# A decoder layer with a selective scan: decays in two SBUF tiles, one scan per step, C's rows in PSUM, normalisation on ScalarE

## The chip, the core and the metric

The kernel runs on one core of a Trainium2 chip. A core has five engines with an instruction queue each: TensorE (PE in the profile; its weight loads are PEld), VectorE (DVE), ScalarE (ACT), GpSimd (POOL) and SyncE (SP), which here only issues DMA transfers. Each engine works through its queue in order; semaphores make one engine wait for another. SBUF is the memory that all engines and the DMA reach, PSUM the small one that TensorE writes its results to. The metric is the time of one execution on the device, in microseconds (us), as the median of several runs.

## What is computed

x is 64 sequences of 128 tokens with 512 channels. Three blocks follow each other, each on a normalised x and added to it: a state-space block (1024 inner channels, 16 states each), an attention block in a band of 64 tokens either way, with a second input that multiplies its result, and a mixture of eight small experts of which two are taken. The part that the change touches most is the first:

```python
def ssm_block(x):                       # x normalised
    h_in, gate = split(x @ in_proj_w.T)
    u   = silu(causal_conv(h_in, 4 taps))
    ts, B, C = split(u @ x_proj_w.T)    # 128, 16, 16 wide
    dt  = softplus(ts @ dt_proj_w.T + dt_proj_b)
    dA  = exp(dt[..., None] * -exp(A_log))
    h_t = dA_t * h_(t-1) + (dt * u)[..., None] * B     # along the tokens
    y   = sum over the 16 states of h * C, plus D * u
    return (y * silu(gate)) @ out_proj_w.T
```

## The kernel before

Two sequences form a group (`GB` = 2, so 256 columns, `TG`); there are 32 groups. The 1024 channels times 16 states of a group are worked off in 32 steps, so 1024 steps in all. Step k belongs to group g, to a block ib of 128 channels and to a quarter j of the states (`where`, line 258). In a step, 128 partitions carry 32 channels times 4 states, and the free dimension 4 quarters of the block times 256 columns, 1024 elements.

A step has these parts, each a function with a line that shows in the profile:

- `loads` (262): once per block, two DMA transfers from scratch in DRAM spread dt (tile dtr) and dt times u (dur) over the partitions. Each has two tiles.
- `by_b` (line 279): GpSimd multiplies dur by B's rows (brep) into h, which has two tiles.
- `decays` (292): ScalarE writes exp(dt A) into da. da lies in PSUM: two halves of 512 elements, one tile each, used by every step again. The first column of each sequence stays zero, which starts the recurrence anew.
- `scan` (300): VectorE runs the recurrence over one half, in place in h. There are two scans per step.
- `by_c` (309): VectorE multiplies h by C's rows (crep, SBUF) into hc; right behind it stand the matmuls that sum over the states into yp (314, 319).
- `gated` (328): once per block VectorE multiplies yp by the gate into y.

All other work is written as four generators, "strands": strand_b makes the next group's inputs (`front`: normalisation, in-projection pin, convolution u, silu th on ScalarE and GpSimd, projections, brep and crep, softplus e, lo, ln, dt), strand_c the gates (pg, gt), strand_a the out-projection po and the attention, strand_t the attention's end (`tail`: o, pw, y2, pc) and the experts. They yield after each piece with a number of ticks to pass and sometimes a condition. The main loop puts eight ticks into every step, and what is due is issued there. So the order on each engine is fixed when the program is built: for step k it is by_b of k+1, first scan, first half of the decays of k+1, two ticks, second scan, second half, gated of k-1, two ticks, by_c with its matmuls, four ticks. One PSUM tile, ps_b, serves one after another most products of the strands; a strand waits with its next product until it is given back (`take_b`, `give_b`).

Normalisation, three times per group: `moments` on VectorE (359, 360), `inv_std` on GpSimd (365, 366), `normalise1` on VectorE (370). In `tail`, ScalarE puts relu(pw + bias) into y2 in SBUF (734) and VectorE multiplies it by en (737). brep and crep are made of two products each (483), copied to SBUF by ScalarE (488).

Of the kernel before, what the change touches and what calls it, by code (L numbers as in the profile page):

```python
# [8 lines left out]
F32 = mybir.dt.float32  # L9
# [61 lines left out]
def decoder_layer_kernel(  # L71
# [34 lines left out]
    ps_d = pool("ps_d", 1, space=PSUM)  # L106
# [138 lines left out]
    da = []  # L245
    for h in range(2):
        t = ps_d.tile([P, 2, GB, P], F32, tag=f"da{h}", name=f"da{h}")
        nc.vector.memset(t, 0.0)
        da.append(t)
# [5 lines left out]
    dtr, dur, hs, yps = {}, {}, {}, {}  # L255
# [19 lines left out]
    def by_b(k):  # L275
        if k < n_steps:
            g, ib, j = where(k)
            hs[k] = work([P, 4, TG], "h", 2, f"h_{k}")
            nc.gpsimd.tensor_tensor(  # L279
                hs[k], dur[g, ib], brep[g][:, j, :].unsqueeze(1).to_broadcast([P, 4, TG]),  # L280
                ALU.mult,
            )

    def decays(k, half):
# [4 lines left out]
        for s in range(2):  # L289
            c = 2 * half + s  # L290
            col = (ib * NJ + j) * 4 + c
            nc.scalar.activation(  # L292
                da[half][:, s, :, 1:], d4[:, c, :, 1:], AF.Exp, scale=acol[:, col : col + 1]
            )

    def scan(k, half):
        if k >= n_steps:
            return
        h = flat(hs[k][:, 2 * half : 2 * half + 2, :])
        nc.vector.tensor_tensor_scan(  # L300
            h, da[half].rearrange("p c b t -> p (c b t)"), h, 0.0, ALU.mult, ALU.add
        )

    def by_c(k):
        if k >= n_steps:
            return
        g, ib, j = where(k)
        h = work([P, 4, TG], "hc", 2, f"hc_{k}")
        nc.vector.tensor_tensor(  # L309
            h, hs.pop(k), crep[g][:, j, :].unsqueeze(1).to_broadcast([P, 4, TG]), ALU.mult  # L310
        )
        if j == 0:
# [11 lines left out]
    def gated(k):  # L324
        g, ib, j = where(k)
        if j == NJ - 1:
            y[g, ib] = work([P, TG], "y", 10, f"y_{g}_{ib}")
# [35 lines left out]
    def inv_std(mv, name):  # L363
        rs = work([P, GB], "rs", 3, f"rs_{name}")
        nc.gpsimd.tensor_scalar(rs, mv[:, :, 1], EPS, None, ALU.add)
        nc.gpsimd.tensor_tensor(rs, rs, nhalf, ALU.pow)
        return rs

    def normalise1(dst, src, mv, rs, b):
        nc.vector.tensor_scalar(  # L370
            dst, src[:, b, :], mv[:, b, 0:1], rs[:, b : b + 1], ALU.subtract, ALU.mult
        )

    def normalise(dst, src, mv, rs):
        for b in range(GB):
            normalise1(dst[:, b, :], src, mv, rs, b)
# [30 lines left out]
    def front(g):  # L407
# [4 lines left out]
        yield 3, None  # L412
        normalise(xf, xf, mv, rs)
# [63 lines left out]
        for sel, lst, nm in ((selb, brep, "brep"), (selc, crep, "crep")):  # L477
            lst[g] = work([P, NJ, TG], nm, 2, f"{nm}_{g}")
            for j2 in range(0, NJ, 2):
                yield 1, free_b  # L480
                ps = take_b(f"p{nm}_{g}_{j2}")
                for j in (j2, j2 + 1):
                    nc.tensor.matmul(
                        ps[:, (j - j2) * TG : (j - j2 + 1) * TG], sel[:, j].rearrange("p i n -> p (i n)"),
                        bc, start=True, stop=True,
                    )
                yield 3, None
                nc.scalar.copy(flat(lst[g][:, j2 : j2 + 2, :]), ps)
                give_b()

        for half in range(2):
# [37 lines left out]
            later(8, to_dram(g, half, dt, e))  # L531

# [8 lines left out]
    def strand_b():  # L541
        for g in range(n_groups):
            yield 1, at((g - 1) * STEPS)
# [25 lines left out]
    def out_proj(g):  # L569
# [21 lines left out]
        yield 4, None  # L591
        body[g] = work([P, GB, H], "body", 1, f"body_{g}")
        normalise(body[g], t, mv, rs)
# [113 lines left out]
    def tail(g, b):  # L707
# [24 lines left out]
        yield 6, None  # L732
        y2 = work([P, H], "y2", 1, f"y2_{n}")
        nc.scalar.activation(y2, pw, AF.Relu, bias=bao)
        give_b()
        yield 4, None
# [227 lines left out]
```

## Time and profile before

| | before |
|---|---|
| median of 3 runs | 7188.0 us (7186.71 to 7194.45) |
| the profiled execution | 7195.22 us, span 7193.5 us |
| granted TensorE clock, mean | 0.829 |
| product with B (line 279), GpSimd | 1024 x 2411 ns |
| decays (292), ScalarE | 4096 x 476 ns |
| scans (300), VectorE | 2048 x 1206 ns |
| product with C (309), VectorE | 1024 x 1466 ns |
| normalisation (370), VectorE | 192 in three rows: 1510, 1518 and 1144 ns on average |
| y times en (737), VectorE | 64 x 1563 ns |

The span is from the first to the last instruction of that one execution. A row of the profile gives the line, the engine, the operation, output and inputs by name, how often it runs, the busy time and the mean duration. A wait names who waited, for whom, for how long in total, how often and at most how long. An engine's busy time counts stretches in which at least one of its instructions runs; consecutive ones can overlap by some 0.08 us (a product with C of 1.23 us started at 3554.63 us, the scan behind it at 3555.77).

### The profile page before, as it was taken

What the parts mean: (1) busy time and instruction counts of PE and PEld (TensorE: products, weight loads), DVE (VectorE), ACT (ScalarE), POOL (GpSimd) and SP (SyncE); (2) the same over time, 40 slices, a digit from 0 to 9 for tenths busy, and PEclk for the clock granted to TensorE, in tenths of its full rate; (3) what the DMA queues carried; (4) which work ended last, traced back from release to release, by engine and by line L of the source; (5) the groups of instructions that cost most, each with busy time, mean ns of one, the idle gap of its engine ahead of it and who ended that gap; (6) DMA issues with size and microseconds to landing.
All of it is one profiled execution on the core that took longest, in us unless ns stands there. A gap on an engine that the chain in (4) does not pass through costs nothing. (4 is left out here: it accounts for less than half of the span.)

```text
span 7193.5 us, 89695 instructions
## 1 busy us (share of the span) xinstructions
PE 5313.9 (74%) x33348; PEld 2932.3 (41%) x33348; DVE 5689.6 (79%) x6834; ACT 3600.1 (50%) x6946; POOL 3810.7 (53%) x1922
## 2 busy tenths in 40 slices
PE   4577777777777777777777777777777777777776
PEld 2344443444444344444444444444443444344433
DVE  3887888888788877888877888877888788888782
ACT  2455445555445554455554455554455544555551
POOL 4655455554455554555554555544555545555540
PEclk7788888888888888888888888888888888888887
DMA  2222222322232322222222223222323222222221
GB/s 80 100 92 83 96 90 98 101 92 81 91 100 95 101 80 90 95 93 95 98 82 94 93 95 101 90 83 89 102 95 100 81 90 95 93 95 97 76 89 34
DMA packets 282614, 651.49 MB, mean 91 GB/s; under 512 B 48960, under 2 KB 116544, under 8 KB 282176
## 3 DMA queue, kind: packets, MB, share of 16 engines
q1 hardware_dynamic: 282176, 645.76, 26.9%
q8 instruction: 262, 4.29, 0.2%
q14 instruction: 176, 1.44, 0.1%
HBM read 558.61 MB, written 85.98 MB: 90 GB/s over the span
## 5 line engine op out<-in xcount | busy, mean ns | idle before, releaser
L279 POOL TENSOR_TENSOR h<-dur,brep 128x1024 f32<-128x1024 f32 x1024 | 2466.6, 2411 | 2345.2 <-DVE hc L309 1641.5
L292 ACT ACTIVATE da<-dtr,acol 128x254 f32<-128x254 f32 x4096 | 1947.0, 476 | 2089.8 <-DVE h L300 1941.6
L300 DVE TENSOR_TENSOR_SCAN h<-da,h 128x512 f32<-128x512 f32 x2048 | 2414.2, 1206 | 228.8 <-ACT da L292 123.6
L309 DVE TENSOR_TENSOR hc<-h,crep 128x1024 f32<-128x1024 f32 x1024 | 1501.4, 1466 | 32.7 <-DVE h L300 0.5
L319 PE MATMUL yp<-hc,sely 128*32 128x256 f32 x8192 | 794.8, 460 | 931.7 <-DVE hc L309 931.4
L387 PE MATMUL pin<-xnT,wi 128*128 128x256 f32 x2048 | 691.9, 511 | 152.0 <-DVE xr L743 124.6
L319 PEld LDWEIGHTS yp<-hc,sely 128*32 128x32 f32 x8192 | 184.9, 117 | 1363.9 <-DVE hc L309 1158.3
L387 PE MATMUL pg<-xnT,wi 128*128 128x256 f32 x2048 | 564.7, 437 | 164.9 <-DVE u L439 157.7
L439 DVE SCALAR_TENSOR_TENSOR u<-pin,cw,u 128x254 f32<-128x254 f32 (+2 forms) x768 | 363.2, 477 | 403.2 <-ACT u L431 385.0
L387 PEld LDWEIGHTS pin<-xnT,wi 128*128 128x128 f32 x2048 | 532.9, 267 | 340.5 <-DVE xr L743 148.6
L655 DVE TENSOR_REDUCE mx<-sq 128x2 f32<-128x512 f32 (+1 forms) x1024 | 565.6, 612 | 26.7 <-PE sq L608 26.6
L387 PEld LDWEIGHTS pg<-xnT,wi 128*128 128x128 f32 x2048 | 441.9, 221 | 288.1 <-issue 194.8
L579 PE MATMUL po<-wo,y 128*128 128x512 f32 x1024 | 517.9, 653 | 0.0
L683 ACT ACTIVATE pe<-sk 128x896 f32<-128x896 f32 x512 | 450.5, 906 | 114.7 <-PE sk L608 114.7
L403 POOL TENSOR_TENSOR th<-th,u 128x512 f32<-128x512 f32 x128 | 185.8, 1452 | 463.8 <-ACT th L401 463.8
L602 PEld LDWEIGHTS <-identb 128*128 128x128 bf16 x2048 | 189.6, 107 | 497.4 <-issue 240.7
L602 PE MATMUL sq<-mask,identb 128*128 128x448 bf16 x1024 | 340.7, 458 | 47.3 <-DVE mx L655 42.4
L602 PE MATMUL sk<-mask,identb 128*128 128x448 bf16 x1024 | 277.0, 380 | 69.6 <-ACT pe L683 68.3
L608 PE MATMUL sq<-kT,qT 16*128 16x192 f32 (+1 forms) x4096 | 325.4, 440 | 0.0
L579 PEld LDWEIGHTS po<-wo,y 128*128 128x128 f32 x1024 | 208.0, 212 | 268.7 <-issue 268.3
L608 PE MATMUL sk<-qT,kT 32*128 32x192 f32 (+1 forms) x4096 | 295.1, 406 | 1.3 <-DMA qT<-nm 1.3
L518 DVE TENSOR_SCALAR lo<-e 128x1024 f32<-128x1024 f32 x64 | 55.1, 861 | 291.0 <-ACT e L513 269.7
(145 smaller groups left out, 6777.9 us busy)
## 6 DMA issues: line engine op xcount, KB each, us to landing
wi<-in_w_inproj SPq DMA_DIRECT2D x257, 512.0 KB
dtr<-dtd SPq DMA_DIRECT2D x256, 512.0 KB
dur<-dud SPq DMA_DIRECT2D x256, 512.0 KB
wo<-in_w_outproj SPq DMA_DIRECT2D x130, 512.0 KB
dtd<-dt SPq DMA_DIRECT2D x256, 128.0 KB
dud<-e SPq DMA_DIRECT2D x256, 128.0 KB
rc<-rd SPq DMA_DIRECT2D x256, 128.0 KB
xf<-in_x SPq DMA_DIRECT2D x64, 256.0 KB
```

Of the source, the lines that this page charges most:

```text
L279: nc.gpsimd.tensor_tensor(hs[k], dur[g, ib], brep[g][:, j, :].unsqueeze(1).to_broadcast([P, 4, TG]), ALU.mult,)
L292: nc.scalar.activation(da[half][:, s, :, 1:], d4[:, c, :, 1:], AF.Exp, scale=acol[:, col : col + 1])
L300: nc.vector.tensor_tensor_scan(h, da[half].rearrange("p c b t -> p (c b t)"), h, 0.0, ALU.mult, ALU.add)
L309: nc.vector.tensor_tensor(h, hs.pop(k), crep[g][:, j, :].unsqueeze(1).to_broadcast([P, 4, TG]), ALU.mult)
L319: nc.tensor.matmul(yps[0][32 * c : 32 * c + 32, :], sely, h[:, c, :], start=False, stop=(j == NJ - 1), skip_group_check=True,)
L387: nc.tensor.matmul(ps[:, s * TG : (s + 1) * TG], w[:, s, k, :], flat3(xnT[g][:, k, :, :]), start=(k == 0), stop=(k == HC - 1),)
L439: nc.vector.scalar_tensor_tensor(uc[:, s, :, d:], hin[:, s, :, : P - d], cw[:, c, KC - 1 - d : KC - d], uc[:, s, :, d:], ALU.mult, ALU.add,)
L579: nc.tensor.matmul(po[:, b, :], y[g, c][:, b * P : (b + 1) * P], w[:, c - c2, :], start=(c == 0), stop=(c == IC - 1),)
L602: nc.tensor.matmul(ps[r // 2][:, r % 2, :PAIR], identb, mask[:, i * EDGE : i * EDGE + PAIR], start=True, stop=False,)
L608: nc.tensor.matmul(ps[r // 2][:, r % 2, c0 : c0 + r1 - r0], left[32 * r : 32 * r + rows, s, blk * P : (blk + 1) * P], right[32 * r : 32 * ...
L655: nc.vector.tensor_reduce(mx[:, blk, h0 : h0 + 2], ps[rp][:, :, c0 : c0 + r1 - r0], AX.X, ALU.max,)
L683: nc.scalar.activation(t, ps[rp][:, :, :PAIR], AF.Exp, scale=0.25)
```

## The change

- da moves from PSUM to SBUF, with one tile of 1024 elements for even steps and one for odd ones. There is one scan per step over all 1024 elements, and one piece of decays (still four instructions).
- The two PSUM tiles so freed hold C's rows. TensorE writes them there once per group (`c_rows`, `rows`): the first pair in a group's last step, the second in the next group's second step. The copies to SBUF go. B's rows are still copied, now in pairs with three tiles, behind the softplus in `front`.
- h gets a third tile and by_b runs two steps ahead. The matmuls over the states become a function of their own (`summed`) and are issued one step later, after the next scan. gated stands behind a third and fourth tick. loads moves to the third step of a block and loads the block after the next.
- Normalisation becomes one ScalarE instruction per sequence, x times rs plus a shift, which a small VectorE instruction makes before. The ticks around it are more.
- In `tail` the relu stays in PSUM (pw), and VectorE reads it there. y has nine tiles instead of ten. strand_b starts three steps earlier.

```diff
+    da = [fixed([P, 4, GB, P], f"da{i}") for i in range(2)]
...
-            hs[k] = work([P, 4, TG], "h", 2, f"h_{k}")
+            hs[k] = work([P, 4, TG], "h", 3, f"h_{k}")
...
+                da[k % 2][:, c, :, 1:], d4[:, c, :, 1:], AF.Exp, scale=acol[:, col : col + 1]
...
+    def scan(k):
+        if k < n_steps:
+            nc.vector.tensor_tensor_scan(
+                flat(hs[k]), da[k % 2].rearrange("p c b t -> p (c b t)"), flat(hs[k]), 0.0,
+                ALU.mult, ALU.add,
+            )
...
-            h, hs.pop(k), crep[g][:, j, :].unsqueeze(1).to_broadcast([P, 4, TG]), ALU.mult
+            hcs[k], hs.pop(k),
+            crep[g, j // 2][:, j % 2, :].unsqueeze(1).to_broadcast([P, 4, TG]), ALU.mult,
         )
+
+    def summed(k):
+        g, ib, j = where(k)
+        h = hcs.pop(k)
...
-            y[g, ib] = work([P, TG], "y", 10, f"y_{g}_{ib}")
+            y[g, ib] = work([P, TG], "y", 9, f"y_{g}_{ib}")
...
+    def shift(mv, rs):
+
+        nc.vector.scalar_tensor_tensor(
+            rs[:, 1, :], mv[:, :, 0], -1.0, rs[:, 0, :], ALU.mult, ALU.mult
         )
...
+    def normalise(dst, src, rs, b):
+        nc.scalar.activation(
+            dst, src[:, b, :], AF.Identity, bias=rs[:, 1, b : b + 1], scale=rs[:, 0, b : b + 1]
+        )
...
+        for jp in range(NJ // 2):
+            yield 1, lambda: free_b() and now[0] >= (g - 1) * STEPS + (STEPS - 3) * jp
+            t = work([P, 2, TG], "brep", 3, f"brep_{g}_{jp}")
+            ps = take_b(f"pbrep_{g}_{jp}")
+            rows(ps.rearrange("p (j t) -> p j t", j=2), selb, g, jp)
+            yield 4, None
+            nc.scalar.copy(flat(t), ps)
...
+    def rows(dst, sel, g, jp):
+
+        for j in range(2):
+            nc.tensor.matmul(
+                dst[:, j, :], sel[:, 2 * jp + j].rearrange("p i n -> p (i n)"), bcs[g],
+                start=True, stop=True,
+            )
+
+    def c_rows(g, jp):
+        if g < n_groups:
+            crep[g, jp] = ps_c.tile([P, 2, TG], F32, tag=f"c{jp}", name=f"crep_{g}_{jp}")
+            rows(crep[g, jp], selc, g, jp)
...
+        nc.scalar.activation(pw, pw, AF.Relu, bias=bao)
+        yield 4, None
         y2 = work([P, H], "y2", 1, f"y2_{n}")
-        nc.scalar.activation(y2, pw, AF.Relu, bias=bao)
+        nc.vector.tensor_tensor(y2, pw, en, ALU.mult)
...
-            if k % NJ == 0 and k:
-                loads(k + NJ)
-            by_b(k + 1)
-            scan(k, 0)
-            decays(k + 1, 0)
+            if k % NJ == 2:
+                loads(k + 6)
+            by_b(k + 2)
+            scan(k)
+            decays(k + 1)
             tick(2)
-            scan(k, 1)
-            decays(k + 1, 1)
+            if k:
+                summed(k - 1)
+            if k % STEPS == STEPS - 1:
+                c_rows(k // STEPS + 1, 0)
+            if k % STEPS == 1 and k > STEPS:
+                c_rows(k // STEPS, 1)
+            tick(2)
             if k:
                 gated(k - 1)
-            tick(2)
             by_c(k)
             tick(TICKS - 4)
```

## The prediction

> **What bounds the kernel now.** I read the page's busy shares first, then the windows, then the waits, then single instructions.
>
> ```profile
> PE 5313.9 (74%) x33348; PEld 2932.3 (41%) x33348; DVE 5689.6 (79%) x6834; ACT 3600.1 (50%) x6946; POOL 3810.7 (53%) x1922
> ...
> 147.00:7022.00 6875.00, 5148.56 (x32576) 2841.64 (x32576) 5617.35 (x6674) 3538.17 (x6845) 3742.87 (x1824) 0.83 0.28 92
> ```
>
> No engine is full; VectorE (DVE) is nearest. The second line is the windows' answer for the stretch between the first and the last step (columns: length, then busy PE, weight loads, DVE, ACT, POOL): 1024 steps in 6875 us, 6.71 us each. DVE is busy 5617 us of it and idle 1258. The ends, 7193.5 - 6875 = 318 us, have no steps. So the loop is DVE's own work plus what DVE waits for, and DVE's waits within that stretch say for whom:
>
> ```profile
> DVE u L439 <- ACT u L431: 352.3, 121, 4.8
> DVE lo L518 <- ACT e L513: 245.0, 61, 6.1
> DVE h L300 <- ACT da L292: 123.6, 70, 3.4
> DVE gt L559 <- ACT gt L557: 113.0, 96, 2.6
> DVE h L300 <- POOL h L279: 78.4, 34, 3.5
> ```
>
> Most of it is ScalarE being late, though ScalarE is half idle. Why it is late stands in the waits of all engines:
>
> ```profile
> ACT da L292 <- DVE h L300: 1941.6, 904, 6.7
> POOL h L279 <- DVE hc L309: 1641.5, 528, 10.2
> PE yp L319 <- DVE hc L309: 931.4, 386, 34.9
> ```
>
> ScalarE's queue is in order. The decays of step k+1 go into the PSUM tile that scan k still reads, so ScalarE stands behind scan k and everything queued after the decays stands with it. TensorE stands in the same way behind the product with C (hc). Both then hand their results to DVE late.
>
> The second cost is inside DVE's busy time:
>
> ```profile
> L309 DVE TENSOR_TENSOR hc<-h,crep x1024: 1191/1225/3339, 146.6 to 7021.0; 128x1024 f32<-128x1024 f32 x171
> L300 DVE TENSOR_TENSOR_SCAN h<-da,h x2048: 1151/1209/1225, 142.7 to 7019.7; 128x512 f32<-128x512 f32 x187
> L737 DVE TENSOR_TENSOR y<-y,en x64: 660/700/2593, 477.1 to 7162.2; 128x512 f32<-128x512 f32 x64
> L586 DVE TENSOR_TENSOR xr<-po,xr x32: 1223/1225/1225, 342.0 to 7041.6; 128x1024 f32<-128x1024 f32 x32
> ```
>
> These are min/median/max in ns. The two operations with both inputs in SBUF (hc; y times en) reach 3.3 and 2.6 us. The two with one input in PSUM (scan; xr+po) never stretch. The timeline shows with what they collide:
>
> ```profile
> 3537.18 2.34 POOL L522 TENSOR_TENSOR lo<-lo,ln 128x1024 f32<-128x1024 f32 x1
> ...
> 3537.61 3.00 DVE L309 TENSOR_TENSOR hc<-h,crep 128x1024 f32<-128x1024 f32 x1
> ```
>
> hc starts while GpSimd (POOL) works and ends 1.1 us after POOL's end at 3539.52: it ran its 1.2 us only then. The two take turns.
>
> **The change, part by part**, against the profiled span of 7193.5 us.
>
> *C into PSUM.* hc then has one input in PSUM; the nearest row is xr+po of the same size, 1225 ns and never longer. hc averages 1466 ns: 1024 x 0.241 = **-247**. Two 0.58 us copies per group leave ScalarE (37 us in all, not on the path). The matmuls are as many as before.
>
> *Normalisation to ScalarE.* Line 370 holds DVE 96.6 + 94.6 + 70.7 = 262 us. The new shift (96 of some 0.17 us, as other [128x2] operations) costs 16: **-246**. ScalarE gains 192 instructions of about 0.65 us (kT with bias: 673 ns), 125 us, hidden while ScalarE is half idle; the price if that cover is gone is the 125 us. The 3 to 5 ticks added around each shift delay only the start of xnT, body and xn, which have a group's time.
>
> *Relu left in PSUM.* y times en averages 1563 ns, the same shape with PSUM input 690 (line 832): 64 x 0.86 = **-55**.
>
> *One scan instead of two.* A pair shows as 2.33 us in the timeline, one alone as 1.21: one start, 0.08 us, goes: 1024 x 0.08 = **-82**.
>
> Together -630.
>
> *Decays in two SBUF tiles.* The gain: ScalarE may write step k+1 once scan k-1 has ended, which DVE finished a step earlier. The ACT-behind-scan wait goes; so does TensorE's wait for hc, since the sums over states of step k-1 are now issued after scan k. What comes next: TensorE's own length (an in-projection of 16 matmuls takes 3.7 to 6.5 us) and the fixed distances in ticks. I take the DVE idle of 1258 down to **550**: u 200, lo 80, da 20, gt 60, h 80, the rest (346 now, small gaps included) 110. That is **-708**; the ends are 250 and 950. ScalarE writing SBUF instead of PSUM shows nowhere in the trace for this shape. The Trainium skill ("ScalarE: Activation LUTs", on an ACTIVATE's destination) says PSUM is the quicker one; nearest rows with SBUF output are 372 to 477 ns for 256 elements against 476 now, and ScalarE has room either way: 0.
>
> *The price.* Now the scan has both inputs in SBUF. No row shows such a scan. The Trainium skill, "SBUF — State Buffer", section "Who interferes with whom", speaks against this change: a DVE instruction with two SBUF inputs and a GpSimd instruction that reads SBUF shut each other out for the whole instruction. The rows above agree for hc. Two values:
> - By the hc row, 0.241 us a step: 247 us. The sum would be 7193.5 - 630 - 708 + 247 = 6103. But hc met POOL rarely, because POOL's next product with B waited for that very hc; and TensorE alone has 5314 us of work.
> - By the rule, counted over one group in the changed order: after a scan (2.25) POOL's product with B holds the way for 2.35 + 0.1, while DVE has by_c (1.14) and whatever else lies there. Five steps of 32 have nothing else (wait 1.3 each), four only the gate's product (1.0), about eight one operation of 0.7 (0.6): 6.5 + 4 + 5 = 16 us. POOL's other work is some 36 us; the softplus chain (lo, dt, e, 20 us) sits in six steps with room for 3: 17 more; th, u and oT 5: 38 us. DVE idles 550/32 = 17 us a group anyway, and I let a third of that lie over these turns: 32 us a group, 1.0 us a step, **+1024**.
>
> I take the second, since POOL's product of step k+2 becomes free just where scan k starts: they meet every step. As a check from below: scans and POOL's own instructions couldn't overlap, so 1024 x 2.25, plus POOL's 3743 less the some 160 by which its means exceed its undisturbed durations (2411 against 2352 for the product with B), plus 318: 6200.
>
> *Moves.* by_b runs two steps ahead with a third h tile. It waits for by_c k-1 and on POOL only the next product stands behind it. The loads of dtr/dur go out two steps later in the block of four, for the block after next. On SyncE the dtr load then waits for the decays one step on; behind it stand wi, wo and the scratch stores. That queue already waits 624 us for the decays and DVE and TensorE show no DMA wait from it above 4 us: 0, at worst some 60 us. gated waits for matmuls issued half a step before instead of one and a half; behind it on DVE stands by_c, which POOL and the matmuls wait for. It shows 3.7 us now; I have 40 of the 110 for it. The row copies of B move behind the softplus chain, a few steps ahead of their use; their third tile keeps the two in use alive. y has nine tiles instead of ten; eight are one group's, and the ninth is due only after the out-projection has begun: 0 for both.
>
> Sum: 7193.5 - 630 - 708 + 1024 = 6880. The profiled run took 7195.2 against a median of 7188: 5.5 us below the span. **Forecast 6875 us**, 4.4% faster.
>
> **Rivals.**
> 1. *Slower: the scan's wait for POOL.* Place: between by_c and scan. Where any vector operation stands there, POOL's product begins first and the scan waits for nearly all of it; in the softplus steps POOL has a queue. From 630 + 708 = 1338 us, 1.31 us a step, it eats the gain. At 1.5 us (1536): 7193.5 - 1338 + 1536 - 5.5 = **7386**. For it: POOL's busy 3.66 us plus a scan of 2.25 is 5.9 of 6.7 us. Against: a waiting DVE gets in after one POOL instruction (hc above did), and DVE goes straight from by_c to the scan in most steps. Idle that doesn't fall (950 instead of 550, at 1.0 us) ends at 7275, on the same side. Chance 0.24.
> 2. *The scan doesn't take turns with POOL.* Then the sum is 5856 and TensorE (5314 busy) sets the time; with an eighth of the span lost around it, as in-order waits, about **6250**. For it: no row of a scan with two SBUF inputs. Against: hc and y times en. Chance 0.10.
> 3. *Gains and turns cancel*: within 0.2% (what a measurement here can tell from no change). Chance 0.04.
>
> The likeliest, 6550 to 7170, has 0.62. Faster 0.62 + 0.10 = 0.72, same 0.04, slower 0.24. The range for 8 in 10 leaves out most of rival 2 and the end of rival 1: 6480 to 7380.
>
> **What would show it.** The scan's row: about 2.25 us at least, mean near 3.2 with a maximum above 4.5, and POOL's product with B stretched towards 4.6. hc near 1225 with no long ones. The wait of the decays for the scan from 1941 to under 300, TensorE's for hc to under 100, DVE idle near 550 in the loop. If the scan's mean is above 3.6, or u and lo still wait 600 us together, the forecast is wrong on the slow side; a mean of 2.3 makes rival 2.

## The result, and the profile after

| | before | after |
|---|---|---|
| median | 7191.23 us (7186.71 to 7200.09) | 7136.73 us (7132.99 to 7137.72) |
| ratio, 95% interval | | 0.992 (0.9905 to 0.9939) |
| profiled execution: time, span | 7195.22, 7193.5 us | 7137.72, 7136.0 us |
| span less VectorE's busy time | 1504 us | 1443 us |

The change makes the kernel 0.8% faster, 54 us, where 4.4% was forecast. First the busy line of the page after the change, and the windows' row from the first to the last step (length, then busy time of PE, weight loads, DVE, ACT and POOL):

```profile
PE 5192.0 (73%) x33348; PEld 2863.5 (40%) x33348; DVE 5692.8 (80%) x5714; ACT 3513.8 (49%) x7074; POOL 5359.2 (75%) x1922
...
147.00:7000.00 6853.00, 5056.82 (x32662) 2786.27 (x32662) 5622.56 (x5569) 3452.26 (x6972) 5287.69 (x1826) 0.85 0.28 93
```

VectorE has 1120 instructions fewer and is as busy as before within 3 us (5689.6). GpSimd does the same 1922 instructions and is busy 1548 us longer. VectorE's idle time in the loop is 1230 us; it was 1258. So two large things happened inside a total that hardly moved.

The first is in the single instructions of the changed kernel (min/median/max in ns; the second line is the page's row of the same scan, with its mean of 2753 ns):

```profile
L295 DVE TENSOR_TENSOR_SCAN h<-da,h x1024: 2259/2664/4439, 135.5 to 6956.0; 128x1024 f32<-128x1024 f32 x171
L295 DVE TENSOR_TENSOR_SCAN h<-da,h 128x1024 f32<-128x1024 f32 x1024 | 2818.8, 2753 | 41.5 <-ACT gt L572 26.4
L305 DVE TENSOR_TENSOR hc<-h,crep x1024: 1157/1209/1223, 141.4 to 6958.4; 128x1024 f32<-128x1024 f32 x171
L277 POOL TENSOR_TENSOR h<-dur,brep x1024: 2331/4201/4438, 133.1 to 6948.3; 128x1024 f32<-128x1024 f32 x171
L754 DVE TENSOR_TENSOR y<-pw,en x64: 676/688/692, 498.3 to 7104.0; 128x512 f32<-128x512 f32 x64
```

hc and y times en have no long instances left. The scan now has them, and GpSimd's product with B lasts 4.2 us in the median where it lasted 2.35. The timeline shows how, in the same kernel:

```profile
3511.90 0.68 DVE L754 TENSOR_TENSOR y<-pw,en 128x512 f32<-128x512 f32 x1
3512.13 2.36 POOL L277 TENSOR_TENSOR h<-dur,brep 128x1024 f32<-128x1024 f32 x1 [3.20 <-DVE hc L305]
3512.50 4.13 DVE L295 TENSOR_TENSOR_SCAN h<-da,h 128x1024 f32<-128x1024 f32 x1
...
3518.32 2.28 DVE L295 TENSOR_TENSOR_SCAN h<-da,h 128x1024 f32<-128x1024 f32 x1
3518.54 21.49 POOL L277 TENSOR_TENSOR h<-dur,brep 128x1024 f32<-128x1024 f32 x5 [4.06 <-DVE hc L305]
```

At 3511.90 a short operation on VectorE lies ahead of the scan. GpSimd's product gets in at 3512.13 and ends at 3514.49. The scan, there since 3512.50, ends 2.14 us after that, about its own length. At 3518.32 the scan comes first and takes 2.28, and now GpSimd waits: its next five products take 21.49 us, 4.3 each.

The second is in the waits. What VectorE waits for in the loop after the change:

```profile
DVE y L329 <- PE yp L320: 222.8, 92, 7.6
DVE lo L511 <- DMA dud<-e: 208.7, 17, 12.6
DVE mx L673 <- PE sq L626: 163.4, 61, 4.6
DVE lo L511 <- DMA dtr<-dtd: 117.3, 10, 12.9
DVE gt L574 <- ACT gt L572: 107.0, 61, 3.4
...
DVE u L445 <- ACT u L437: 26.8, 34, 4.0
```

u (352 before) and the waits for decays and h (202 before, 15 now) are gone as forecast. In their place stand the gate's product y (4 before), lo, now waiting for a store to DRAM and no longer for ScalarE, and mx (11 before). Of lo's 374 us in the loop, 209 are put down to the store dud, 117 to the load dtr and 46 to ScalarE. The waits of all engines in the changed kernel:

```profile
POOL h L277 <- DVE hc L305: 973.1, 255, 9.6
ACT da L289 <- DVE h L295: 656.3, 355, 7.3
PE yp L320 <- DVE hc L305: 434.1, 182, 27.7
```

ScalarE's wait for the scan fell from 1942 to 656 us and TensorE's for hc from 931 to 434. VectorE lost only 28 us of idle time by it.

### The profile page after: what moved, and what is told of

It reads as the page before. It is cut to its first block, busy times and chain, and to the rows that moved or that the text cites. A ratio compares the mean times of both kernels' runs of the same rounds, so it can differ in the third digit from the quotient of the medians.

```text
span 7136.0 us, 88821 instructions
## 1 busy us (share of the span) xinstructions
PE 5192.0 (73%) x33348; PEld 2863.5 (40%) x33348; DVE 5692.8 (80%) x5714; ACT 3513.8 (49%) x7074; POOL 5359.2 (75%) x1922
## 5 line engine op out<-in xcount | busy, mean ns | idle before, releaser
L277 POOL TENSOR_TENSOR h<-dur,brep 128x1024 f32<-128x1024 f32 x1024 | 3443.2, 3377 | 1074.0 <-DVE hc L305 973.1
L295 DVE TENSOR_TENSOR_SCAN h<-da,h 128x1024 f32<-128x1024 f32 x1024 | 2818.8, 2753 | 41.5 <-ACT gt L572 26.4
L289 ACT ACTIVATE da<-dtr,acol 128x254 f32<-128x254 f32 x4096 | 1736.3, 498 | 679.5 <-DVE h L295 656.3
L305 DVE TENSOR_TENSOR hc<-h,crep 128x1024 f32<-128x1024 f32 x1024 | 1237.5, 1208 | 20.5 <-DVE sm L734 0.2
L390 PE MATMUL pin<-xnT,wi 128*128 128x256 f32 x2048 | 536.7, 422 | 103.9 <-issue 72.2
L390 PEld LDWEIGHTS pin<-xnT,wi 128*128 128x128 f32 x2048 | 431.3, 213 | 222.8 <-issue 153.9
L406 POOL TENSOR_TENSOR th<-th,u 128x512 f32<-128x512 f32 x128 | 319.2, 2494 | 86.9 <-ACT th L404 86.8
L494 PE MATMUL pz<-ts,wdt 128*128 128x256 f32 x512 | 182.6, 489 | 275.9 <-ACT dt L503 268.8
L437 ACT ACTIVATE u<-pin,cb,cw 128x256 f32<-128x256 f32 x256 | 130.4, 559 | 424.9 <-PE pin L390 424.9
L749 PE MATMUL pw<-oT,wao 128*128 128x512 f32 x256 | 181.8, 849 | 182.0 <-POOL oT L745 182.0
```

The lines of the kernel that those rows point to most:

```text
L277: nc.gpsimd.tensor_tensor(hs[k], dur[g, ib], brep[g, j // 2][:, j % 2, :].unsqueeze(1).to_broadcast([P, 4, TG]), ALU.mult,)
L289: nc.scalar.activation(da[k % 2][:, c, :, 1:], d4[:, c, :, 1:], AF.Exp, scale=acol[:, col : col + 1])
L295: nc.vector.tensor_tensor_scan(flat(hs[k]), da[k % 2].rearrange("p c b t -> p (c b t)"), flat(hs[k]), 0.0, ALU.mult, ALU.add,)
L305: nc.vector.tensor_tensor(hcs[k], hs.pop(k), crep[g, j // 2][:, j % 2, :].unsqueeze(1).to_broadcast([P, 4, TG]), ALU.mult,)
L390: nc.tensor.matmul(ps[:, s * TG : (s + 1) * TG], w[:, s, k, :], flat3(xnT[g][:, k, :, :]), start=(k == 0), stop=(k == HC - 1),)
L406: nc.gpsimd.tensor_tensor(th, th, t, ALU.mult)
```

## Experiments

All ratios are to the kernel before on the same chip (7190 to 7194 us), each with an interval of about 0.2% either way. "Idle" is the span less VectorE's busy time. The quoted texts are what was expected of each run; a "theory" in them is one of the explanations that the run was to tell apart, and "the half" is the second softplus half.

| | edit | us | ratio | DVE busy | idle |
|---|---|---|---|---|---|
| after | | 7137 | 0.992 | 5693 | 1443 |
| e1 | after, scan's first input from PSUM | 6637 | 0.923 | 5162 | 1478 |
| e2 | after, gate's product later | 7290 | 1.013 | 5857 | 1429 |
| e7 | after, one decays tile | 7660 | 1.065 | 5602 | 2052 |
| e11 | after, two h tiles | 7443 | 1.035 | 6019 | 1421 |
| e13 | after, decays in SBUF halves, two scans | 7993 | 1.111 | 7019 | 972 |
| e10 | after, normalisation and relu as before | 7609 | 1.058 | 5993 | 1618 |
| e17 | after, sums right behind by_c | 7532 | 1.048 | 5660 | 1876 |
| e6 | before + normalisation and relu as after | 6993 | 0.972 | 5377 | 1615 |
| e14 | e6 + late sums and gate | 7339 | 1.020 | 5413 | 1939 |
| e15 | after, memories as before | 7428 | 1.032 | 5276 | 2162 |
| e18 | e15, sums right behind by_c | 7563 | 1.052 | 5283 | 2265 |
| e3 | after, second softplus half later | 6935 | 0.964 | 5823 | 1107 |
| e4 | e3 + gate later + pw later | 6896 | 0.959 | 5783 | 1108 |
| e9 | e3 + pw later | 7114 | 0.989 | 5850 | 1262 |
| e8 | e3, sums two ticks earlier | 7019 | 0.976 | 5779 | 1247 |
| e12 | e3, sums right behind by_c | 7331 | 1.019 | 5755 | 1567 |
| e5 | before, second softplus half later | 7522 | 1.046 | 5619 | 1903 |
| e16 | e15, second softplus half later | 7241 | 1.007 | 5391 | 1847 |

### The price of the turns

**e1.** The scan's first input is one value of C's rows in PSUM, repeated; the decays are still written and waited for (the last value of the tile is the start value). The recurrence's factor and its new start at each sequence are left out.

```diff
-    flat(hs[k]), da[k % 2].rearrange("p c b t -> p (c b t)"), flat(hs[k]), 0.0,
-    ALU.mult, ALU.add,
+    flat(hs[k]), crep[cg, cj // 2][:, cj % 2, 0:1].to_broadcast([P, 4 * TG]), flat(hs[k]),
+    da[k % 2][:, 3, 1, P - 1 : P], ALU.min, ALU.add,
```

> The changed kernel, but the scan takes its first input from PSUM (one value of C's rows, repeated) instead of the decays in SBUF; the decays are still written, and one element of them is the scan's start value, so every wait stays. The decays' factor and the zero at each sequence start are left out of the result. Theory 1 (scan and GpSimd shut each other out, and GpSimd's lateness makes the new idle time): the scan's mean falls from 2753 to about 2270 ns, GpSimd's busy time from 5359 to about 3850 us, the waits of lo for its tile (374 us in the loop) and of mx for sq (163 us) to under 150 us together; time 6200 to 6400 us. Theory 2 (only the order is at fault: the sums over states are issued too late, GpSimd's lateness costs nothing but the scan's own stretch): idle time stays near 1230 us in the loop, time 6600 to 6700 us. Theory 3 (TensorE bounds it): the stretch comes back as waits for TensorE, time above 6850 us.

Measured: 6637 us, 500 below after. The rows of the scan and of GpSimd's product in e1:

```profile
L296 DVE TENSOR_TENSOR_SCAN h<-crep,da,h x1024: 2317/2343/2351, 136.5 to 6462.5; 128x1024 f32<-128x1024 f32 x171
...
L277 POOL TENSOR_TENSOR h<-dur,brep x1024: 2337/2355/2417, 134.1 to 6455.6; 128x1024 f32<-128x1024 f32 x171
```

With one input in PSUM neither is ever stretched. So the turns are a matter of where the scan's inputs lie, and their price in this kernel is 500 us. VectorE's idle time did not fall with them: it is 1246 us in the loop (6333 us less 5087 busy) against 1230. That is the second theory's figure, in time and in idle. The new waits are not made by the turns; lo waits 374 us in both kernels.

**e2.** The gate's product goes to the end of the step, just ahead of the next scan.

```diff
-            if k:
-                gated(k - 1)
             by_c(k)
             tick(TICKS - 4)
+            if k:
+                gated(k - 1)
```

> The changed kernel, but the gate's product of step k-1 is issued at the end of step k instead of ahead of by_c. Theory 2 (the sums over states are issued too late for it): the wait of y for yp falls from 223 us to under 30 us and the time by 120 to 220 us, to about 6920 to 7020 us. Theory 3 (TensorE is behind in any order): the wait turns up at by_c, po or the next product; time within 40 us of 7137.

Measured: 7290, slower by 154; both theories missed. The wait of y fell from 223 to 50 us, and the scan's mean rose from 2753 to 2918 ns, 169 us in all:

```profile
L295 DVE TENSOR_TENSOR_SCAN h<-da,h 128x1024 f32<-128x1024 f32 x1024 | 2988.3, 2918 | 137.9 <-ACT da L289 100.3 <-ACT gt L572 26.7 <-POOL h L277 10.9
```

A VectorE operation between by_c and the scan lets GpSimd's product in first. That is the mechanism of the prediction's first rival, at one place.

### One part of the change taken back

**e7.** One decays tile in SBUF for every step instead of two.

```diff
-    da = [fixed([P, 4, GB, P], f"da{i}") for i in range(2)]
+    da = [fixed([P, 4, GB, P], "da0")] * 2
```

> The changed kernel with one decays tile in SBUF for all steps instead of two. ScalarE then can't write step k+1 before scan k has ended, as before the change. If the second tile is what the change gains by, VectorE waits for the decays in most steps without other work (some 1.0 us in 20 of 32) and stands behind a late ScalarE elsewhere: 7600 us or above, with the wait of u for ScalarE back above 200 us. If ScalarE's lead is worth little, since the idle time is set elsewhere: below 7350 us.

**e11.** Two h tiles, and by_b one step ahead.

```diff
-            hs[k] = work([P, 4, TG], "h", 3, f"h_{k}")
+            hs[k] = work([P, 4, TG], "h", 2, f"h_{k}")
...
-            by_b(k + 2)
+            by_b(k + 1)
```

> After, with two h tiles and GpSimd's product one step ahead instead of two. Theory 1 (the third tile is what lets GpSimd's product meet the scan in every step): with two tiles the product waits for the product with C again, starts behind it at the same moment as the scan, takes turns as before, and is late for the next scan: scan waits for the product over 300 us together, 7300 or more. Theory 2 (two steps ahead is more than is needed): within 1% of 7136, with the scan's mean lower and its wait for the product below 150.

**e13.** Decays in two half tiles in SBUF, each used by every step, and two scans per step, as before the change.

```diff
-            scan(k)
-            decays(k + 1)
+            scan(k, 0)
+            decays(k + 1, 0)
             tick(2)
+            scan(k, 1)
+            decays(k + 1, 1)
```

> After, with the decays as two half tiles in SBUF that every step uses again and two scans per step, as before, but in SBUF. Theory 1 (joining the scans took what the second tile gives back: the halves already let ScalarE write one half while the other is read): within 2% of after, 7000 to 7280, far below the 7660 of one joined tile. Theory 2 (the second full tile gives more than halves can): 7450 or more, with the wait of the decays for the scan above 1500 us again.

**e10.** Normalisation on VectorE and relu into SBUF, each undone as in the diff of the change.

> After, with normalisation back on VectorE and the relu back in SBUF. Theory 1 (the parts add): this part alone took 200 us from before and the rest of the change added 144, so the time is about 7194 + 144 = 7340 (7290 to 7390). Theory 2 (the parts help each other: an operation on VectorE between two scans lets GpSimd's product in first, so removing such operations is worth more after than before): 7400 or more, with the scan's mean above 2.85 us. If the offload brings nothing once the loop is bound by turns: 7136 to 7200.

Measured: 7660, 7443, 7993 and 7609, so 523, 307, 856 and 472 us above after. Every part is worth much where it stands. e7 is where its larger figure lay, but not in the places named: u waits 129 us (above 200 was expected) and the scan waits 173 us for the decays (some 640 were expected), while gt, y and lo wait over 300 each. In e11, which takes back the third tile and the second step ahead together, the scan's wait for h rose from 12 to 420 us and its mean to 3050 ns, as the first theory said. In e10 the part is worth 472 us though it is worth 200 in the kernel before (e6, below), as the second theory said, but the scan's mean (2813 ns) stayed below the 2.85 us it asked for: 300 us are VectorE's busy time, 175 idle. e13 went against its first theory: the halves do not do what the second full tile does. The half scans' row of e13, and ScalarE's wait for them:

```profile
L298 DVE TENSOR_TENSOR_SCAN h<-da,h x2048: 1189/1876/3346, 136.5 to 7816.5; 128x512 f32<-128x512 f32 x187
...
ACT da L290 <- DVE h L298: 3130.6, 1570, 9.4
```

A half scan starts twice per step and is shut out twice: 2101 ns on average, 4.2 us per step against 2.75 for the joined scan. Joining the scans, costed in the prediction at one start (82 us), is worth far more once both inputs lie in SBUF: e7 and e13 both use their decays tiles again in every step, and e13 with two scans is 333 us slower.

### The change built up from before

**e6.** Before, with normalisation on ScalarE and the relu left in PSUM, as in the diff of the change.

> The kernel before, with the normalisation on ScalarE and the relu left in PSUM, nothing else of the change. If VectorE's work is what the loop's time follows, the 300 us that leave VectorE (line 370 and the product with en, less the shifts) leave the time: 6890 to 6950 us. If the work only stood where VectorE would have waited for ScalarE or TensorE anyway (the idle time is set by chains through the other engines), VectorE's idle time rises by half of it or more: 7030 us or above.

**e14.** e6, with the sums over the states and the gate's product issued where the change has them; decays in PSUM, two h tiles.

```diff
+            if k:
+                summed(k - 1)
             scan(k, 1)
             decays(k + 1, 1)
+            tick(2)
             if k:
                 gated(k - 1)
-            tick(2)
             by_c(k)
```

> Before, with normalisation on ScalarE, the relu in PSUM, and the sums over the states (and the gate's product) where the change issues them; decays in PSUM, C's rows in SBUF, two h tiles. Theory 1 (the sums' place brings in PSUM what it brings in SBUF, 396 us): 6992 - 300 to 400, so 6590 to 6700, with TensorE's wait for hc falling from 1740 (weights and matmuls) below 800. Theory 2 (idleness of an early engine; waits reappear): 6940 to 7050.

**e15.** After, with the memories swapped back: decays in two PSUM halves with two scans (as in e13), C's rows copied to SBUF behind B's. All the rest stays: three h tiles, by_b two steps ahead, the places of loads, row copies, sums and gate, the earlier start of strand_b.

```diff
-    da = [fixed([P, 4, GB, P], f"da{i}") for i in range(2)]
+    da = []
+    for h in range(2):
+        t = ps_c.tile([P, 2, GB, P], F32, tag=f"da{h}", name=f"da{h}")
...
             brep[g, jp] = t
+            yield 1, free_b
+            t = work([P, 2, TG], "crep", 4, f"crep_{g}_{jp}")
+            ps = take_b(f"pcrep_{g}_{jp}")
+            rows(ps.rearrange("p (j t) -> p j t", j=2), selc, g, jp)
```

> After, with the decays back in two PSUM halves (two scans) and C's rows back in SBUF (copied by ScalarE); normalisation on ScalarE, three h tiles, late sums and their order stay. Theory 1 (the swap of memories costs more by the scan's turns with GpSimd, some 500, than it brings by hc's, some 250, and one scan start, 82): 170 us or more below after, 6800 to 6970, scan pair near 2.4 us, hc's mean 1.4 to 1.7 us. Theory 2 (with two h tiles ahead hc now meets GpSimd in every step as the scan did, so the turns only change place): 7080 to 7300, hc's mean above 1.8 us. The forecast's own reading (swap frees 708 of idle): 7400 or more.

Measured: 6993, 7339, 7428. The first part alone brings 200 us, between the two figures expected: VectorE's busy time falls by 313 and its idle time rises by 111. Both theories of e14 missed. The last, the swap of memories, brings 291 (e15 to after), and inside it VectorE's busy time rises by 417 while its idle time falls from 2162 to 1443, by **718**. Both theories of e15 fell: it is at 7428, where the forecast's own reading had put it. What lies between, 435 us slower from e6 to e15, is the order of the work: the moves, which the prediction had at nothing, and the late sums. VectorE's longest waits in the loop of e15:

```profile
DVE lo L515 <- DMA dud<-e: 565.2, 29, 20.6
DVE u L449 <- ACT u L441: 468.7, 92, 9.9
DVE y L333 <- PE yp L324: 369.7, 173, 5.6
```

In e6 these are 0 (its lo waits 90 us, for ScalarE), 205 and 113. The largest is lo of a group's second softplus half. Its output takes a tile that the first half's e still holds, and e is held until its store (dud) has landed. ScalarE's ln stands there in the same way for the tile of the first half's dt, until the store dtd has landed. Why the store is late stands on SyncE's queue in e15, around one such wait:

```profile
3385.61 1.19 SPq L727 DMA_DIRECT2D sd<-oT  x2
3386.89 0.39 SPq L736 DMA_DIRECT2D en<-in_enc  x1
3388.03 0.33 SPq L739 DMA_DIRECT2D sm<-sd  x1
3396.40 0.57 SPq L270 DMA_DIRECT2D dtr<-dtd  x1
3397.06 0.56 SPq L270 DMA_DIRECT2D dur<-dud  x1
3397.67 3.85 SPq L559 DMA_DIRECT2D dtd<-dt  x4
3401.62 5.65 SPq L559 DMA_DIRECT2D dud<-e  x4
```

```profile
3390.90 1.01 ACT L292 ACTIVATE da<-dtr,acol 128x254 f32<-128x254 f32 x2
...
3395.36 1.01 ACT L292 ACTIVATE da<-dtr,acol 128x254 f32<-128x254 f32 x2
...
3408.51 1.28 ACT L514 ACT_TABLE_LOAD   x1 [11.63 <-DMA dtd<-dt]
...
3414.16 0.69 DVE L515 TENSOR_SCALAR lo<-e 128x1024 f32<-128x1024 f32 x1 [20.08 <-DMA dud<-e]
```

The load of dtr stands at the head of SyncE's queue from 3388.4 until the last decays that read its tile end at 3396.37. The stores stand behind it. GpSimd had made e by 3390.4; its store is issued from 3401.62, and VectorE, which was ready at 3394.08, stands still until 3414.16 with scans behind it. The load accounts for some 9 of these 20 us (an estimate: dt was made at 3382.86, so the stores could have begun at 3388.4 instead of 3397.67); the rest comes from the eight stores' own issue, 9.6 us, and the 6.9 us from its end to lo.

The load stands so early for a reason that the program shows. Before, it went out four steps ahead of the block that it fetched, two steps after the last decays that read its tile had been issued. Now it goes out six steps ahead, and in the same step those decays are issued only after it (`loads(k + 6)` stands ahead of `decays(k + 1)`). SyncE's waits in e15 show that a long wait of this load is the rule:

```profile
SPq L270 <- ACT da L292: 1047.8, 141, 27.2
SPq L270 <- ACT oT L724: 976.7, 52, 21.9
SPq L270 <- ACT va L666: 899.8, 61, 22.9
```

The names oT and va are what ended last by the profile; in the stretch above it was the decays, the readers of dtr. Under all names together the load waits 2930 us in e15, 672 before, 454 in e6 and 2026 in after. The row for the decays alone, before and after:

```profile
SPq L270 <- ACT da L292: 624.3, 46, 22.5
```

```profile
SPq L268 <- ACT da L289: 1504.6, 165, 30.1
```

So the load's wait tripled in after too, but there it is not what holds lo. The kernel after, around one of lo's waits:

```profile
3460.49 4.35 POOL L517 TENSOR_TENSOR dt<-dt,lo 128x1024 f32<-128x1024 f32 x1
3464.91 4.35 POOL L520 TENSOR_TENSOR e<-dt,u 128x512 f32<-128x512 f32 x2
```

```profile
3468.07 3.69 SPq L552 DMA_DIRECT2D dud<-e  x4
3474.89 0.57 SPq L268 DMA_DIRECT2D dtr<-dtd  x1
```

```profile
3479.24 0.69 DVE L511 TENSOR_SCALAR lo<-e 128x1024 f32<-128x1024 f32 x1 [12.26 <-DMA dud<-e]
```

The load is behind the store here. GpSimd's dt takes 4.35 us where it took 2.40 on average before, by its turns with the scans, so e is ready late; the store ends its issue at 3471.76, and lo begins 7.5 us later. From the first half's lo (3445.42) to the moment when VectorE is ready for the second there are 21.6 us, against 28.2 in a group before (3503.47 to 3533.66, less 2.03 of wait). VectorE comes earlier, the store later. But GpSimd's lateness is not what the wait hangs on, for e1, where the turns are gone, has it as well:

```profile
DVE lo L512 <- DMA dud<-e: 242.8, 20, 12.8
DVE lo L512 <- ACT da L289: 109.5, 9, 12.7
```

In a group of e1 dt takes 2.39 us and e is ready 16.3 us after the first lo (23.8 in the group of after), and still the second lo waits 12.45: VectorE is there 19.0 us after the first, and the store ends its issue at 23.5, with lo 7.9 us behind it. What both groups share is that VectorE is there when the store of e is only being issued, and from the start of that issue until lo it takes 11.2 us (after) and 12.5 us (e1).

**e17 and e18.** The sums right behind their product with C, as before the change, in after and in e15.

```diff
-            if k:
-                summed(k - 1)
...
             by_c(k)
+            if k < n_steps:
+                summed(k)
```

> After, with the sums right behind their product with C and nothing else. Theory 1 (the place and the memories belong together; with decays in SBUF the late place brings some 400): 7136 + 300 to 450, so 7440 to 7590, y's wait for yp gone, those of gt, u and rmx up by 400 or more together. Theory 2 (the 396 of e12 were that kernel's strands): 7060 to 7250.

> The kernel of e15 (memories as before, the rest as after) with the sums right behind their product with C. Theory 1 (with decays in PSUM the late place costs some 350, nearly all of it the gate's wait for yp): 7428 - 350, so 7000 to 7150, y's wait of 351 below 50. Theory 2 (the 346 of e14 were that kernel's strands): 7350 to 7550.

| | sums behind by_c | sums a step later |
|---|---|---|
| decays in PSUM halves (e18, e15) | 7563 | 7428 |
| two decays tiles in SBUF (e17, after) | 7532 | 7137 |

The late sums bring 396 us in after, as the first theory of e17 said, and 136 with the old memories, where the first theory of e18 expected a loss; the swap brings 291 with late sums and 31 without. The two need each other. So e14's loss of 346 is not what late sums cost in general. In both kernels with decays in PSUM the wait of y for yp rises with them, from 113 to 445 us (e14) and from 163 to 370 (e15); in e15 those of mx and rmx fall by some 300, in e14 nothing falls by as much. And e18 against e6 has the memories and the sums of before in both, and is **570 us slower**: third h tile and by_b two ahead, places of loads, row copies and gate, strand_b's start. (One piece of e18 stands neither in before nor in after: C's copies to SBUF behind the softplus chain.) The third tile with by_b two ahead helps in after (e11). Of the rest only the place of the loads shows itself, on SyncE's queue and in lo's wait for the store, 580 us in e18; none was tried alone, so its share of the 570 us is argued and not shown.

### Distances in the strands

**e3.** The second softplus half starts 16 ticks later.

```diff
         for half in range(2):
+            if half:
+                yield 16, None
```

> The changed kernel, but the second half of the softplus chain starts 16 ticks (two steps) later. If the wait of lo is GpSimd's and the stores' lateness against a fixed distance in ticks (theory 1), lo's wait in the loop falls from 374 us to under 80 us and the time by 200 to 300 us, to about 6840 to 6940 us. If the chain only moves the jam on (theory 3, or GpSimd full), the scan's waits for h or its stretch rise by as much; time within 60 us of 7137.

**e4.** e3, with the gate as in e2, and pw 8 ticks later.

```diff
         nc.gpsimd.tensor_tensor(flat(o), flat(o), flat(rc), ALU.mult)
-        yield 6, free_b
+        yield 14, free_b
```

> The changed kernel with the gate's product at the end of the step, the second softplus half 16 ticks later, and the attention's output product pw 8 ticks later behind GpSimd's product oT. Theories 1 and 2 together (each new wait of VectorE is a distance in ticks that GpSimd's or TensorE's piece has outgrown): the waits of y, lo and mx (760 us in the loop) fall to under 200 us, time about 6600 to 6750 us. Theory 3: other waits for TensorE take their place, time above 7000 us.

**e9.** e3 with the later pw alone.

> After, with the second softplus half 16 ticks later and pw 8 ticks later, the gate's product where the change has it. Theory 1 (the gate's product between the product with C and the scan lets GpSimd in first, as the gate placed late alone cost 1.3%): this is faster than the kernel with all three shifts (6896) by about the half of what the late gate cost, since there the late gate paid for itself partly in the wait for yp: 6850 to 6890, y's wait near 240, mx's under 20. Theory 2 (waits move on): pw's 160 us only move to other operations: 6900 to 6950, as with the half alone (6935).

**e8 and e12.** e3, with the sums two ticks earlier, and right behind by_c.

> The changed kernel with the second softplus half 16 ticks later (the version that took 6935 us) and the sums over states of step k-1 issued right behind scan k and the decays, two ticks earlier. If the wait of y for yp comes from TensorE's pieces of those two ticks (projections of 3.7 us) standing in front: y's wait falls from 245 us to under 100 us, time about 6790 to 6860 us. If TensorE is late from the ticks before: y's wait stays above 180 us and the time within 40 us of 6935.

> After with the second softplus half 16 ticks later, and the sums over the states issued right behind their product with C, as before the change. Theory 1 (the prediction's: issuing them a step later spares TensorE's queue the stand behind the product with C, and so VectorE's waits for strands): TensorE's wait for hc rises from some 790 us (weights and matmuls together) above 1200, waits of gt, mx, xr and u grow by over 100 us together, 7000 or more. Theory 2 (that stand was idleness of an early engine): the time is within 0.5% of 6935 (the kernel with the half alone), y's wait of 245 us falls below 50 and as much reappears elsewhere; or it is faster by up to that 245.

**e5 and e16.** The edit of e3 in the kernel before, and in e15.

> The kernel before, with the second softplus half 16 ticks later and nothing else. Theory A (the distance between the halves was already too short, and VectorE waited there too, put down to ScalarE's e): lo's wait in the loop falls from 245 us to under 100 us and the time by 80 to 150 us, to about 7040 to 7110 us. Theory B (only the change's faster steps brought VectorE to lo too early): the time stays within 40 us of 7191.

> The kernel of e15 with the second softplus half 16 ticks later. Theory 1 (the store of the first half holds the tile that lo needs, as in after, where this brought 200): 100 to 250 below e15. Theory 2 (as in before, where the same shift cost 330, SyncE's queue is then held up where the decays' PSUM halves let the loads go a step later): same as e15 or slower.

One line brings 201 us in after (e3) and 187 in e15 (e16): lo then finds its tile free, its wait goes from 374 us to 2 in e3 and from 621 to about 160 in e16. In the kernel before, where no such store is waited for, the same line costs 330 us (e5). No theory of e5 had that. The wait that is new there:

```profile
DVE sm L718 <- DMA sm<-sd: 206.7, 30, 8.2
```

The second half's stores now stand on SyncE's queue right ahead of the transfers that sm waits for (2 us before), and the waits of the scans for decays and h grew from 202 to 321, that of lo for ScalarE from 245 to 311. That the stores cost e5 its time is not shown: sm waits 150 us in e6 too, which is faster than before.

e4 lies between the figures of its theories. e12 shows the late sums once more, 396 us again, and where the time goes without them. TensorE's waits for hc in e12, weights and matmuls:

```profile
PEld yp L320 <- DVE hc L305: 1141.4, 489, 8.6
PE yp L320 <- DVE hc L305: 890.5, 346, 7.7
```

In e3 they are 446 and 344. The wait of y falls from 245 to under 15 us, and those of gt, u, mx and rmx, which TensorE feeds through its queue, rise by 197, 254, 134 and some 160. In e8, where both expectations missed, two ticks were enough to trade 79 us of y for 105 of gt and 105 of rmx.

e9 is a miss of all theories: e3 with one piece of the attention 8 ticks later is 179 us slower, with u waiting 287 us (28 in e3) and y 346; e4, which has the late gate as well, is the fastest of all at 6896. So the shifts do not add. The strands hand one PSUM tile from one to the next, and a piece that comes later changes who has it next. In e9 TensorE's pw waits 104 us for VectorE's gt and pc 129 us for its u; in e3 neither waits for these at all. Why e4, where the same two wait 63 and 70 us, is fast is open. e4 is 3.4% faster than after and 4.1% than before.

## Why the prediction was wrong

It was right in direction and wrong in size: 4.4% forecast, 0.8% measured. Its sum was -630 (work off VectorE), -708 (idle) and +1024 (turns), -314 in all. Measured on the profiled spans: busy time +3 where +394 was forecast, idle -61 where -708 was. The busy time came out 391 us better and the idle time 647 worse, so the right direction is what two larger errors left over, and luck.

- **Work off VectorE, -630.** hc has no long instance, y times en is 688 ns, normalisation is gone: right for these. The shift was costed at 16 us for 96 of them. It has two SBUF inputs and takes turns too: 32 of 1826 ns and 32 of 1083 ns, 93 us in two of its three rows.
- **Turns, +1024: the mechanism right, the size too large.** The Trainium skill ("SBUF — State Buffer", "Who interferes with whom") spoke against the change, and the scan's maximum of 4439 ns and e1 confirm it. But the scan's mean is 2753 ns and not 3200: 0.49 us a step over its minimum, 506 us, where 1.0 us a step was taken. With the 630 gone and the busy time unchanged, all turns together took about 633 us (an estimate). Half of the scans last 2664 ns or less, 0.40 above the minimum, and GpSimd pays the rest of the turns (its product is 4201 ns in the median). Which of the counts was too large, the 16 us of a group for the product with B or the 22 for GpSimd's other work, was not separated. The other value, 247 by the hc row, was too small by 259 and so nearer to the scan's 506 than the one that was taken.
- **Idle, 1258 to 550: the step that failed.** It measured 1230. Term by term: u 27 (200 forecast), da 2 (20) and h 13 (80) are better than forecast; gt is 107 (60), lo 374 (80), and the rest 707 where 110 was taken, with y for yp 223, xr 200 and mx 163 in it. ScalarE's wait for the scan, put under 300, is 656, and TensorE's for hc, put under 100, is 434. The reason given, decoupling, was not wrong: with all else as after, the swap of memories with its second tile takes idle from 2162 to 1443 (e15), 718 us, and the late sums bring 396 us of time (e17). What failed, as far as the runs show, is the part named **Moves**, put at "0, at worst some 60 us": by_b two ahead, loads two steps later in the block (which is two steps earlier before their use), row copies moved. strand_b's start three steps earlier got no figure at all. With before's memories and sums all this costs 570 us (e6 to e18), and idle time rises by 650 (1615 to 2265). The prediction did name SyncE's queue and what stands behind the load of dtr, "the scratch stores"; it took the absence of waits for that queue in the trace of before as a sign that it had room. In e15 and e18 those stores behind the load are the longest wait of VectorE. In after the load is behind the stores (in the group shown), but VectorE comes too early for them: lo was forecast at 80 us and waits 374, with the turns and without (e1). One strand moved by 16 ticks gives 201 of it back (e3).
- **The gate.** 40 us were kept for its wait for yp. It is 223; with the gate later it is 50, and the time is no better for it (e2).
- **What was said to show the forecast wrong** (a scan mean above 3.6, or u and lo at 600 together) did not occur: 2.75 and 401. The lost time was in waits that this sign did not watch: y, mx, xr.
- **Rivals.** The first has its place (e2), not its size. The second, no turns, is out by e1; even with the turns gone the time is 6637, not 6250, because the idle time stays. (Its sum is off by a little: 5314 us with an eighth lost around it are 6073, or 6213 if the eighth is of the old span. In the first rival, 950 in place of 550 gives 7274.) The third, gains and turns cancel, came nearest: 54 us of 7191 are left, for another reason than it gave.

What is not settled: which of the moves costs how much of the 570, what they cost together with the new memories (there only e11 and e17 took one back, and both were slower), and why e5 loses what e3 wins. That would need each move by itself. Nor was the granted TensorE clock separated: it goes from 0.790 (e13) to 0.865 (e1), and is 0.829 before and 0.843 after. It does not order TensorE's work by itself: a matmul of pin lasts 392 ns on average in e9, at 0.818, and 422 in after.

## What to carry to other kernels

Before a wait is counted as gained, ask which wait the engine reaches next. In a hand-ordered kernel, moving an issue is an edit like any other and needs a figure of its own; here the moves together cost 570 us with the old memories. A queue that nobody waits for today is no sign of room: read what stands behind the waiting instruction and when it will be needed. Putting both inputs of a VectorE operation into SBUF beside a busy GpSimd had a price here (500 us by e1) that depended on who started first; let nothing stand between the operation that releases GpSimd and the long one.

## What the runs showed of the hardware

- A scan of 128x1024 with both inputs in SBUF and GpSimd at work: 2259 to 4439 ns. With one input in PSUM: 2317 to 2351 ns (e1, with a minimum in place of the product), so that undisturbed the SBUF form is even a little shorter. In two halves: 4.2 us per step instead of 2.75.
- Even a [128x2] operation takes turns: the shift of norm a takes 161 ns at least and 1900 in the median.
- From the end of the issue of a store of e to the lo that takes its tile there were 7.5 us in the group of after, 7.9 in that of e1 and 6.9 in that of e15.
- ScalarE's decays into SBUF have a median of 494 ns against 477 into PSUM (e15): 4096 of them make 70 us of ScalarE, unseen in the time. The Trainium skill ("ScalarE: Activation LUTs", "Step-by-step: what each stage is for") says that PSUM is the quicker destination, and the rows agree. One normalisation of 128x512 on ScalarE took 806 to 814 ns in the median where 650 was estimated.
